# Tying indirect gathers to VectorE's message products, four to one, in a graph layer on one core

## The chip, the cores and the metric

The kernel runs on one core of one Trainium2 chip. The metric is the device time of one execution in microseconds (us). The engines are named as in the profile: PE is TensorE's matmul (PEld its weight loads), DVE is VectorE, ACT is ScalarE, POOL is GpSimd, and SP is SyncE, which only issues transfers here.

## What is computed

One message-passing layer of a graph network: 12,500 nodes of 128 features and 400,000 edges, sorted by destination. An edge's filter W comes from its length; the message is the projected source row times W; messages are summed by destination; two small matrices, a residual and a layer norm end it.

```python
rbf = jnp.exp(-(distances[:, None] - centers) ** 2 / (2.0 * width * width))
cut = 0.5 * (jnp.cos(jnp.pi * distances / CUTOFF) + 1.0) * (distances <= CUTOFF).astype(h.dtype)
W = (jax.nn.silu(rbf @ fw1 + fb1) @ fw2 + fb2) * cut[:, None]
messages = (h[src] @ pw + pb) * W
agg = jax.ops.segment_sum(messages, dst, num_segments=num_atoms)
return h + (jax.nn.silu(agg @ mw1 + mb1) @ mw2 + mb2)
...
x = _layernorm(x + _L0_gnn_ref(x, edge_index, edge_weight, ...), axis=-1)
```

Edges longer than the cutoff add nothing. The lengths go up to about 56 where the cutoff is 10, so most edges fall away.

## The kernel before

**Stages.** First the edges are packed: on VectorE, for seven chunks of the edge list, the edges beyond the cutoff are squeezed out and the rest are written to tables of sources (`srci`), destinations (`dl`) and lengths. In the first 100 us the rows of x are also projected with `pw` and stored to a table `proj` in HBM. The packing of later chunks is strewn over the next 500 us.

**Quads.** The edges that remain are worked on in 139 groups of 512, called quads here (q = 0 to 138; `NL` is 139, `QT` is 4, `QE` is 512). A quad takes:

- four **gathers** (`fetch`, line 1093, the indirect DMA at line 1099): each brings 128 source rows of 512 bytes into one quarter j of a buffer. GpSimd issues them in order. Quads 0 to 11 gather from x and are projected afterwards; from quad 12 on (`FROM_X`) they gather from `proj`.
- the **filter**: `basis` (ACT), `first` (PE, line 1167), `silu` (ACT, line 1173), `second` (PE, lines 1182 and 1185), which leaves the filter of the quad in a PSUM bank.
- the **product** (`message`, line 1189, the multiplication at line 1201): VectorE multiplies the filter by the gathered rows. It waits for the four gathers, and it frees the gather buffer and the PSUM bank.
- `place` (line 1209, the instructions at line 1214): four VectorE instructions that build the matrix that sorts edges by destination, one quad ahead.
- `sum_up` (PE, line 1235), which adds the messages by destination, and `add` (VectorE, line 1269), which puts the sums into `aggT`.

The loop at line 1593 runs over the quads; in the body, `message(q)` comes first, then `second(q + 2)`, `first`, `sum_up(q)`, `place(q + 1)` and the `add` of earlier quads. From quad 70 on the finished nodes' matmuls, statistics and stores are mixed in (`nodes`, `node_first` and so on), and the last seven quads are written out by hand from line 1668 on.

**When a gather may start.** The gather buffers are 21, and 9 from quad 63 on (`LATER`), so a gather could go as soon as the product nine quads earlier has freed its buffer. It is held back further, by a **tie**. The build counts VectorE's instructions of the kinds in `VECTORS` as they are written (`logged`, list `vectors`). `pace(q, j)` (line 449) turns a table (`PACE`) into the number of the VectorE instruction after which gather j of quad q is to start, by a straight line between the table's points and less a correction (`WERE`). Gathers that the planner has allowed stand in `queue`; `gathers()` (line 455) is called after products, after each instruction of `place` and `add` and between packing steps, and writes the first of the queue into the program once `len(vectors)` has come to its pace. `fetch` then adds a dependence on that very instruction (lines 1102 to 1105), so that GpSimd waits for VectorE to have done it. `gathers(must)` forces out what is needed for the quads below `must`: the product of quad q has `must` at q + 1, and `house(q)`, in the last seven quads, at q + 4.

Early on the table asks for a gather some 15 to 20 quads before its product; by quad 100 the distance has shrunk to about two quads, and it stays there.

Of the kernel before, what the change touches and what calls it, by code (L numbers as in the profile page):

```python
# [43 lines left out]
NL = 139  # L44
# [14 lines left out]
FIRST = 16  # L59
LISTS = 5  # L60
PACE = ((2, 17), (3, 26), (4, 36), (5, 54), (7, 95), (9, 125), (10, 144), (12, 170), (18, 250), (24, 324), (30, 373), (36, 458), (42, 544), (48, 612), (54, 691), (60, 754), (66, 826), (72, 902), (78, 982), (84, 1071), (90, 1139), (96, 1218), (102, 1306), (108, 1357), (114, 1414), (120, 1461), (126, 1518), (132, 1580), (138, 1646), (139, 1666))
VECTORS = ("TensorScalarPtr", "TensorTensor", "CopyPredicated", "TensorReduce", "TensorCopy",
           "BNStats")
SPILL = 4
# [27 lines left out]
def kernel(  # L92
# [339 lines left out]
    def place_of(q):  # L432
        n, later = LATER
        return q % len(quad_sb) if q < n else later[(q - n) % len(later)]
# [2 lines left out]

        return max((m for m in range(q) if place_of(m) == place_of(q)), default=-1)

    vectors, queue = [], []  # L440

    def logged(i):

        if i.engine == mybir.EngineType.DVE and str(i.opcode) in VECTORS:
            vectors.append(i.name)
# [3 lines left out]
    def pace(q, j):  # L449

        (a, u), (b, v) = next((k for k in zip(PACE, PACE[1:]) if q < k[1][0]))
        n = int(u + (v - u) * (q + j / QT - a) / (b - a))
        return n - sum(1 for w in WERE if w < q - 2)

    def gathers(must=0):

        while queue and (queue[0][0] < must or len(vectors) >= pace(*queue[0])):
            q, j = queue.pop(0)
            fetch(q, js=(j,))

    def room(q):

        n = q
        while n < NL and before_it(n) < q:
            n += 1
        return n

    def fetches(until, most):

        while fetched[0] < QT * min(most, known[0]) and pool[0] <= until:  # L470
            q, j = divmod(fetched[0], QT)
            if q < FROM_X:
                fetch(q, table=x, js=(j,))
            else:
                queue.append((q, j))
            if j == 0:
                pool[0] = max(pool[0], summed.get(before_it(q), 0.0))
            if j or q not in SINGLY:
                pool[0] += 1.29
            there_at[q] = pool[0] + 2.2  # L480
            fetched[0] += 1
# [5 lines left out]
    def columns(c, nodes, r_d, first, D, CAP, at_i):  # L487
# [31 lines left out]
        yield 0.6  # L519
        fetches(clock[0] + (4.0, 5.0, 5, 25)[min(c, 3)], most[0])  # L520
        gathers()
        sent.add(c)
        pool[0] = max(pool[0], clock[0]) + 1.35
# [510 lines left out]
    def own(q, name, also):  # L1034

        k = q % (4 if q >= OWN_4 else 2)
        if k > 1:
            return quad_sb[OTHERS[2 * also + k - 2]]
        if (name, k) not in own_sb:
            own_sb[name, k] = keep.tile([P, QT, H], F32, name=f"{name}{k}")  # L1040
        return own_sb[name, k]
# [51 lines left out]
    def fetch(q, idx=None, table=None, js=range(QT)):  # L1093
        got = quad_sb[place_of(q) if q >= 0 else 0]
        for j in js:
            if q in SINGLY and j == 0:
                continue
            i = srci[:, 2 * q + j // 2, j % 2:j % 2 + 1] if idx is None else idx[:, j:j + 1]
            g = nc.gpsimd.indirect_dma_start(  # L1099
                out=got[:, j, :], out_offset=None, in_=proj if table is None else table,  # L1100
                in_offset=bass.IndirectOffsetOnAxis(ap=i, axis=0))
            if PACE[0][0] <= q < NL:
                tc.add_manual_dep(
                    g.ins, vectors[min(pace(q, j), len(vectors)) - 1],
                    mybir.DependencyInfo(mybir.DependencyClass.Sync, mybir.DependencyReason.DATA))
        got_of[q] = got

# [81 lines left out]
    def message(q, js=(0, QT)):  # L1189
        gathers(q + 1)  # L1190
        msg = own(q, "msg", 0)
        a, b = js
        if q in SINGLY and a == 0:
            act = q in BY_ACT
            k = (BY_ACT if act else BY_SP).index(q)
            assert q in alone and all(s[0] != q for s in singles[act])
            nc.vector.wait_ge(row_sem[act][k % ROW_SEMS], 16 * P * (k // ROW_SEMS + 1))
            m = nc.vector.tensor_mul(msg[:, 0, :], pu_of[q][:, :H], alone.pop(q))
            tc.declare_no_dep(m.ins, group="rows", reason="waits on row_sem")
            a = 1  # L1200
        nc.vector.tensor_mul(msg[:, a:b, :], pu_of[q].rearrange("p (j f) -> p j f", j=QT)[:, a:b, :],  # L1201
                             got_of[q][:, a:b, :])
        if b == QT:
            free.append(pu_of.pop(q))
            got_of.pop(q)
        gathers()
        return msg

# [384 lines left out]
    for q in range(NL - 7):  # L1593
        while todo and q + 2 >= DIRECT // QT and todo[0] <= chunk_of(min(q + 2, NQ - 1)):
            go_on(todo[0])
        msg = message(q)
        nodes(q)
        most[0] = room(q)
# [71 lines left out]
    q = NL - 7  # L1670
    house(q)
    msg = message(q)
    second(q + 2)
    sum_up(q, msg)
# [9 lines left out]
    q += 1  # L1684
    house(q)
    msg = message(q)
    second(q + 2)
    first(octs(q - 1))
# [49 lines left out]
    p, q = NL - 2, NL - 1  # L1738
# [46 lines left out]
    def more(q):  # L1785

        fetch(-2, srci[:, 2 * q:2 * q + 2, :].rearrange("p r j -> p (r j)"))
        radial(-1, near_d[2 * q:2 * q + 2].rearrange("(o p) e -> o (p e)", o=1))
        basis(-1)
        first(-1)  # L1790
        silu(-1)
        second(-2)
        pu_of[q], got_of[q] = pu_of.pop(-2), got_of.pop(-2)
        place(q)
        msg = message(q)
        pa_of["two"] = ps.tile([P, 2, 2 * W], F32, name="sums", bufs=2)
        sum_up(q, msg)
        base_of(q)
        add(q)
# [95 lines left out]
```

## Time and profile before

| | |
|---|---|
| three runs | 941.90, 944.31, 945.89 us; median 944.31 us |
| the profiled execution | 950.38 us, of which the span from first to last instruction is 948.8 us |
| busy, PE / DVE / ACT / POOL | 663.7 / 565.9 / 398.0 / 539.2 us |
| gathers from `proj` into gather buffers | 412, of 951 ns each on POOL; 96 more, of 952 ns, into the buffers named x |
| products (line 1201) | 142 instructions, in 138 quads whole and in the last quad in four parts |
| mean granted TensorE clock | 0.808 of full speed |

A line of the timeline gives the start in us, the busy time in us, the engine, the source line, the operation, what it writes and reads, how many it stands for, and in brackets the idle time of that engine before it and what ended it. "remote" and "issue" mark waits whose end the profile can't put down to an instruction.

### The profile page before, as it was taken

The numbers are of one execution on the slowest core, as the hardware profiler recorded it, in microseconds if no ns is written. First come the engines' busy times: TensorE is split into PE (matmuls) and PEld (weight loads), VectorE is DVE, ScalarE is ACT, GpSimd is POOL, SyncE is SP. The second block draws the span as 40 slices with busy tenths as digits, with TensorE's granted clock in tenths as the row PEclk, the third lists the DMA queues.
The fourth block names the chain that finished last, engine by engine and source line by source line (L and its number), as shares of the span: only waits on it lengthen the run. The fifth ranks groups of instructions, "written<-read, shape, count | busy, mean of one in ns | idle before, by whom it ended". The sixth has DMA issues, their size and how long they took to land.

```text
span 948.8 us, 11718 instructions
## 1 busy us (share of the span) xinstructions
PE 663.7 (70%) x3531; PEld 517.3 (55%) x3531; DVE 565.9 (60%) x1725; ACT 398.0 (42%) x567; POOL 539.2 (57%) x577
## 2 busy tenths in 40 slices
PE   4663737749778867767767786868796675777656
PEld 3552535537556755655555564646575554554444
DVE  8356638745778767767678584646553344443536
ACT  4432622316335443534334433634643542454235
POOL 6346355565556656666666465546565566664661
PEclk8677767778778878888978898769987787778778
DMA  7574421232233223232324122432422342232222
GB/s 243 161 222 154 147 96 34 77 92 81 62 79 120 71 62 82 69 108 77 94 64 136 54 68 67 120 100 67 142 63 63 105 122 67 65 111 81 70 75 74
DMA packets 51295, 91.23 MB, mean 96 GB/s; under 512 B 12928, under 2 KB 18656, under 8 KB 51226
## 3 DMA queue, kind: packets, MB, share of 16 engines
q0 software_dynamic: 18096, 37.30, 15.6%
q1 hardware_dynamic: 22868, 35.09, 11.2%
q10 hardware_dynamic: 10262, 18.05, 6.0%
q8 instruction: 29, 0.48, 0.2%
q14 instruction: 40, 0.33, 0.1%
HBM read 74.59 MB, written 15.79 MB: 95 GB/s over the span
## 4 chain that ended last, share of the span: by engine, by line
PE 42%; another core or an unknown queue 16%; issue 13%; DVE 13%; ACT 10%; DVEq 1%; DMA 1%; ACTq 0%
PE ph L1167 11%; PE bank L1185 9%; PE sums L1235 9%; PE bank L348 5%; DVE hot L1214 3%; PE bank L1182 3%; PE bank L1283 2%; DVE msg L1201 2%; ACT s L1173 2%; ACT rbf L1151 2%; PE bank L1003 1%; PE bank L345 1%; ACT rbf L1155 1%; DVE aggT L1269 1%
## 5 line engine op out<-in xcount | busy, mean ns | idle before, releaser
L1099 POOL DMA_INDIRECT quad<-proj,srci x412 | 391.7, 951 | 274.0 <-issue 86.1
L1185 PEld LDWEIGHTS bank<-fw_sb,s 128*128 128x128 f32 x1112 | 177.1, 225 | 90.2 <-issue 83.6
L1173 ACT ACTIVATE s<-ph 128x1024 f32<-128x1024 f32 x70 | 71.2, 1017 | 335.6 <-PE ph L1167 159.9
L1167 PE MATMUL ph<-rbf,w_sb 102*128 102x512 f32 x278 | 164.1, 719 | 51.7 <-ACT s L1173 35.7
L1185 PE MATMUL bank<-fw_sb,s 128*128 128x128 f32 x1112 | 180.1, 310 | 22.5 <-issue 22.2
L1214 DVE TENSOR_SCALAR hot<-iota_n,dl,cut 128x80 f32<-128x80 f32 (+4 forms) x408 | 111.1, 338 | 107.0 <-PE sums L1235 49.6
L1235 PEld LDWEIGHTS sums<-hot,msg 128*128 128x128 f32 x816 | 121.5, 218 | 61.3 <-issue 40.3
L1235 PE MATMUL sums<-hot,msg 128*128 128x80 f32 (+4 forms) x816 | 122.5, 299 | 17.3 <-DVE msg L1201 10.1
L1099 POOL DMA_INDIRECT x<-proj,srci x96 | 91.4, 952 | 66.4 <-issue 21.3
L1167 PEld LDWEIGHTS ph<-rbf,w_sb 102*128 102x128 f32 x278 | 57.3, 229 | 99.7 <-issue 58.8
L1269 DVE TENSOR_TENSOR aggT<-aggT,sums 128x80 f32 (+4 forms) x209 | 53.9, 258 | 94.1 <-remote 33.8
L1182 PE MATMUL bank<-fb_b,ones_b 96*128 96x512 bf16 x139 | 60.3, 434 | 49.6 <-DVE msg L1201 15.2
L1201 DVE TENSOR_TENSOR msg<-bank,quad 128x512 f32<-128x512 f32 x78 | 53.2, 682 | 46.2 <-remote 32.7
L348 PEld LDWEIGHTS bank<-pw_sb,xT 128*128 128x128 f32 (+1 forms) x292 | 47.2, 232 | 59.0 <-issue 40.3
L1099 POOL DMA_INDIRECT quad<-in_x_dram,srci x48 | 46.3, 965 | 33.9 <-issue 12.6
L1235 PE MATMUL sums<-quad,quad 128*128 128x128 f32 (+3 forms) x296 | 49.4, 309 | 15.8 <-issue 15.2
L1151 ACT ACTIVATE rbf<-d_sb,rbf_bias,rbf_scale 102x512 f32<-102x512 f32 x70 | 56.1, 801 | 0.0
L1235 PEld LDWEIGHTS sums<-quad,quad 128*128 128x128 f32 x296 | 45.0, 225 | 20.1 <-issue 18.8
L348 PE MATMUL bank<-pw_sb,xT 128*128 128x128 f32 (+1 forms) x292 | 48.5, 319 | 6.2 <-ACT xT L1005 5.6
L345 PE MATMUL bank<-pb_b,ones_b 96*128 96x512 bf16 (+2 forms) x38 | 16.8, 443 | 46.4 <-ACT xT L1005 29.0
L1201 DVE TENSOR_TENSOR quad<-bank,quad 128x512 f32<-128x512 f32 (+1 forms) x40 | 25.9, 647 | 38.0 <-DMA quad<-proj,srci 24.2
L1005 ACT COPY xT<-bank 128x512 f32<-128x512 f32 (+1 forms) x37 | 21.3, 580 | 63.5 <-remote 49.0
(278 smaller groups left out, 881.7 us busy)
## 6 DMA issues: line engine op xcount, KB each, us to landing
d_sb<-near_d ACTq DMA_DIRECT2D x67, 256.0 KB
x<-in_x_dram SPq DMA_DIRECT2D x46, 256.0 KB
quad<-proj,srci POOLq DMA_INDIRECT x412
proj<-hp SPq DMA_DIRECT2D x24, 256.0 KB
out_dram<-x SPq DMA_DIRECT2D x22, 256.0 KB
x<-proj,srci POOLq DMA_INDIRECT x96
r_d<-in_edge_weight_dram SPq DMA_DIRECT2D x5, 256.0 KB
r_dst<-in_dst_dram SPq DMA_DIRECT2D x5, 256.0 KB
```

The costliest lines, as they stand in the source:

```text
L345: nc.tensor.matmul(to[:m, a:a + c, :], ones_b[:, :m], bias_b[:, :c, :], start=True, stop=False)
L348: nc.tensor.matmul(to[:m, k, :], lT[:, k * P:k * P + m], w, start=False, stop=(k == a + c - 1))
L1099: g = nc.gpsimd.indirect_dma_start(out=got[:, j, :], out_offset=None, in_=proj if table is None else table, in_offset=bass.IndirectOffsetO ...
L1151: a = nc.scalar.activation(rbf[:u], d[:u], AF.Square, bias=rbf_bias[:u], scale=rbf_scale[:u])
L1167: nc.tensor.matmul(ph[:, h, :], w1_sb[:2 * KR, h, :], rbf[:2 * KR], start=True, stop=True)
L1173: nc.scalar.activation(s[:, :n], ph[:, :n], AF.Silu)
L1182: nc.tensor.matmul(pu, ones_b[:, :P], bias_b["fb2"].rearrange("k j f -> k (j f)"), start=True, stop=False)
L1185: nc.tensor.matmul(pu[:, j * H:(j + 1) * H], s[:, j * P:(j + 1) * P], fw2_sb, start=False, stop=(j == QT - 1))
L1201: nc.vector.tensor_mul(msg[:, a:b, :], pu_of[q].rearrange("p (j f) -> p j f", j=QT)[:, a:b, :], got_of[q][:, a:b, :])
L1214: nc.vector.tensor_scalar(hot[:, j, :wide(q)], iota_n[:, :wide(q)], dl[:, at[0], at[1]], cut[:, at[0], at[1]], op0=OP.is_equal, op1=OP.mult)
L1235: nc.tensor.matmul(pa[:, k * W:k * W + wide(q)], msg[:, j, :], hot[:, j, :wide(q)], start=(j % n == 0), stop=(j % n == n - 1))
L1269: nc.vector.tensor_add(to, to, pa[:, k * W:k * W + wide(q)])
```

## The change

A gather is no longer tied to the VectorE instruction that its pace names, but to a product. The build keeps a list `products` with the count of VectorE instructions at each whole product. With `HALF = 6`, a gather of pace n is written into the program as soon as the last product's count is at least n - 6, or, if none has come by then, when n + 6 instructions have been written. It is tied to the first product whose count is at least n - 6, or, where there is none yet, to the last product before. Gathers written before the first product get no tie; these are the ones for quads 2 to 11, whose ties to early instructions fall away. Everything else stays: the table, the correction, the planner, the order of the gathers, their buffers and VectorE's instructions.

```diff
+HALF = 6
...
-    vectors, queue = [], []
+    vectors, queue, products = [], [], []
...
     def gathers(must=0):
-        while queue and (queue[0][0] < must or len(vectors) >= pace(*queue[0])):
+        while queue and (queue[0][0] < must or products[-1:] >= [pace(*queue[0]) - HALF]
+                         or len(vectors) >= pace(*queue[0]) + HALF):
             q, j = queue.pop(0)
             fetch(q, js=(j,))
+
+    def tied_to(q, j):
+
+        n = pace(q, j) - HALF
+        return vectors[next((k for k in products if k >= n), products[-1]) - 1]
...
-            if PACE[0][0] <= q < NL:
+            if PACE[0][0] <= q < NL and products:
                 tc.add_manual_dep(
-                    g.ins, vectors[min(pace(q, j), len(vectors)) - 1],
+                    g.ins, tied_to(q, j),
                     mybir.DependencyInfo(mybir.DependencyClass.Sync, mybir.DependencyReason.DATA))
...
         if b == QT:
             free.append(pu_of.pop(q))
             got_of.pop(q)
+            products.append(len(vectors))
         gathers()
```

## The prediction, made before the changed kernel was run

> **What bounds the kernel now.** I read the page first, then the waits of the product, then the waits of PE in the stage where gathers come latest, then single stretches of the timeline.
>
> ```profile
> PE 663.7 (70%) x3531; PEld 517.3 (55%) x3531; DVE 565.9 (60%) x1725; ACT 398.0 (42%) x567; POOL 539.2 (57%) x577
> PEclk8677767778778878888978898769987787778778
> PE 42%; another core or an unknown queue 16%; issue 13%; DVE 13%; ACT 10%; DVEq 1%; DMA 1%; ACTq 0%
> L1099 POOL DMA_INDIRECT quad<-proj,srci x412 | 391.7, 951 | 274.0 <-issue 86.1
> ```
>
> PE leads the chain that ended last, with 42%. POOL is idle 43% of the span, so the ties hold the gathers back, not its speed. DMA has 1% of the chain. Whether a tie matters must show at the products, so I asked what they wait for. Up to quad 98 the rows land long before: the last gather of quad 97 and its product are
>
> ```profile
> 669.14 0.94 POOL L1099 DMA_INDIRECT quad<-proj,srci  x1 [0.30 <-issue]
> 680.16 0.68 DVE L1201 TENSOR_TENSOR msg<-bank,quad 128x512 f32<-128x512 f32 x1
> ```
>
> 11.0 us apart, the least of quads 12 to 98. From quad 99 on they come close. The view of line 1201 from 690 to 870 us (quads 100 to 127):
>
> ```profile
>   DMA quad<-proj,srci: 26.1, 11
> who waited for it (us, times):
>   POOL quad L1099: 9.8, 8
> ```
>
> The longest waits of PE in the same stretch:
>
> ```profile
> PE sums L1235 <- issue: 14.8, 13, 2.4
> PE bank L1185 <- issue: 12.7, 9, 2.3
> PE ph L1167 <- ACT s L1173: 5.0, 1, 5.0
> ```
>
> And busy times by stretches (PE, PEld, DVE, ACT, POOL; then granted clock, DMA share and GB/s):
>
> ```profile
> 690.00:870.00 180.00, 132.19 (x687) 102.74 (x686) 78.64 (x259) 79.56 (x109) 105.55 (x113) 0.81 0.30 87
> 712.00:721.00 9.00, 2.44 (x9) 1.54 (x8) 0.67 (x3) 3.55 (x5) 4.81 (x6) 0.66 0.34 103
> 721.00:734.00 13.00, 13.00 (x67) 10.04 (x68) 7.91 (x28) 4.29 (x5) 7.86 (x9) 0.84 0.15 37
> 797.00:810.00 13.00, 12.93 (x70) 10.13 (x70) 7.78 (x25) 1.62 (x2) 8.80 (x10) 0.88 0.16 42
> ```
>
> This is the heart of it. Eleven products wait 26.1 us for gathers, yet nobody but POOL itself waits for those products: PE does not. PE alternates between stretches in which it is full (13.00 of 13 us) and halts in which it waits for nothing that the profile names (2.44 of 9 us, at a granted clock of 0.66). VectorE is busy 78.64 of 180 us and runs ahead of PE in both.
>
> **The change part by part.** I worked out each gather's tie from the code and the count of VectorE's instructions: 508 gathers from quad 12 on, now tied to 492 different instructions, would hang on 135 products; 298 would be free over 0.3 us earlier than now, 142 over 0.3 us later, 0.8 us earlier in the mean.
>
> *Waits on POOL.* A gather keeps one wait whatever it is tied to:
>
> ```profile
> L1099 POOLq EVENT_SEMAPHORE  x113: 17/17/17, 690.5 to 868.3; - x113
> ```
>
> 17 ns each, and gathers one behind another start 0.94 + 0.30 = 1.25 us apart with it. Gain taken: 0.
>
> *The start.* The first product is at 121.6 us. Gathers of quads 12 to 16 that now begin at 104.7 us would wait for it, 18 hang on it, and POOL needs 18 x 1.25 = 22.5 us to catch up. The first of them and the product of quad 12:
>
> ```profile
> 104.74 0.94 POOL L1099 DMA_INDIRECT quad<-proj,srci  x1 [3.47 <-DMA proj<-hp]
> 237.98 0.67 DVE L1201 TENSOR_TENSOR msg<-bank,quad 128x512 f32<-128x512 f32 x1
> ```
>
> 133 us of cover: 0. Without it, 17 us. The seven packing scatters on POOL's queue wait for nothing new: a gather ahead of one is tied to a product that VectorE does before the scatter's own data. From there to quad 98 no gather would start more than 5.4 us later than it does, against a cover of 11.0 - 2.7 = 8.3 us at least (2.7 is start to product, below): 0.
>
> *Quads 99 to 133.* Here I took VectorE's times as they stand and gave each gather the later of two starts: 1.25 us after the gather before it, or 0.3 us after its product's end. The product can start 2.7 us after the last gather's start, as in the first and third rows here:
>
> ```profile
> 727.45 0.94 POOL L1099 DMA_INDIRECT quad<-proj,srci  x1 [0.30 <-issue]
> ...
> 730.16 0.69 DVE L1201 TENSOR_TENSOR quad<-bank,quad 128x512 f32<-128x512 f32 x1 [4.82 <-DMA quad<-proj,srci]
> 730.16 1.04 PE L1235 MATMUL sums<-hot,msg 128*128 128x104 f32 x8
> ```
>
> Nine products would come later: quads 101 (0.4), 105 (2.0), 113 (0.9), 115 (0.7), 117 (2.0), 118 (0.4), 119 (1.1), 121 (1.0) and 125 (0.5), 9.0 us in all. About as many would come up to 0.7 us earlier, 2.4 us in all. The two largest show the pattern, a last gather that moves from an instruction before a pair of products to the first of the pair:
>
> ```profile
> 717.39 0.94 POOL L1099 DMA_INDIRECT quad<-proj,srci  x1 [0.30 <-issue]
> 721.03 0.69 DVE L1201 TENSOR_TENSOR msg<-bank,quad 128x512 f32<-128x512 f32 x1 [8.29 <-remote]
> 722.61 0.69 DVE L1201 TENSOR_TENSOR msg<-bank,quad 128x512 f32<-128x512 f32 x1
> 727.33 0.38 PE L1182 MATMUL bank<-fb_b,ones_b 96*128 96x512 bf16 x1
> ...
> 793.37 0.94 POOL L1099 DMA_INDIRECT quad<-proj,srci  x1 [0.30 <-issue]
> 797.24 0.69 DVE L1201 TENSOR_TENSOR msg<-bank,quad 128x512 f32<-128x512 f32 x1 [7.94 <-remote]
> 798.89 0.68 DVE L1201 TENSOR_TENSOR msg<-bank,quad 128x512 f32<-128x512 f32 x1
> 804.04 0.38 PE L1182 MATMUL bank<-fb_b,ones_b 96*128 96x512 bf16 x1
> ```
>
> Quad 105's last gather has pace 1328 and starts at 717.39; its new tie is instruction 1330, the product of quad 104, done at 721.7. So it starts at 722.0, and the product at 724.7 instead of 722.61. What is late next? `second` of quad 107, at 727.33, which needs the bank that this product frees at 723.3: 4.0 us of slack for 2.0 us. At quad 117 it is 804.04 - 799.6 = 4.5 us for 2.0. The other seven have 2.3 us or more for at most 1.1. So PE covers all nine. Taken: 0; bounds -2.4 and +9.0 us, if PE had no slack.
>
> *VectorE beside the gathers.* Releases would fall on `place`, which often follows the product. Rows of both kinds, each with the gather that starts during it or just before:
>
> ```profile
> 475.25 1.10 DVE L1214 TENSOR_SCALAR hot<-iota_n,dl,cut 128x112 f32<-128x112 f32 x4
> 475.60 0.94 POOL L1099 DMA_INDIRECT quad<-proj,srci  x1 [1.74 <-DVE hot L1214]
> ...
> 748.69 1.06 DVE L1214 TENSOR_SCALAR hot<-iota_n,dl,cut 128x104 f32<-128x104 f32 x4
> 749.28 1.04 POOL L1099 DMA_INDIRECT quad<-proj,srci  x1 [4.66 <-DVE hot L1214]
> 750.26 1.34 DVE L1214 TENSOR_SCALAR quad<-iota_n,dl,cut 128x104 f32<-128x104 f32 x4
> 750.62 0.94 POOL L1099 DMA_INDIRECT quad<-proj,srci  x1 [0.30 <-DVE quad L1214]
> ```
>
> 475.60 is a gather that is tied to a product already: `place` took 1.10 us, 0.04 above 1.06. The worst case is 1.34, 0.28 above. With 135 releases and VectorE's 13% of the chain: 135 x 0.04 x 0.13 = 0.7 us, at most 135 x 0.28 x 0.13 = 4.9, at least 0 (as many may hit it now). Taken: 0.7, since the row at 475 is the very case.
>
> [...]
>
> *The end.* From quad 134 on gathers are forced out and would be tied 4 us or more earlier, with cover either way. Quad 129's product waits 1.79 us for its rows; its last gather would start 0.3 us earlier, and PE did wait there:
>
> ```profile
> 878.15 0.69 DVE L1201 TENSOR_TENSOR msg<-bank,quad 128x512 f32<-128x512 f32 x1 [1.79 <-DMA quad<-proj,srci]
> 878.90 0.38 PE L1182 MATMUL bank<-fb_b,ones_b 96*128 96x512 bf16 x1 [0.22 <-DVE msg L1201]
> ```
>
> Taken: -0.3, bounds -1.8 and 0.
>
> *The sum.* 0 + 0 + 0 + 0.7 - 0.3 = +0.4 us on the profiled execution's 950.38 us. That execution lies 6.1 us (0.6%) above the median of the runs; carried over to the median, 944.31 + 0.4 is 944.7 us, no change. What this kernel's measurement can tell from no change is about 0.5%, 4.7 us.
>
> **The rivals.**
>
> *Slower: bursts reach PE.* One release now frees up to four gathers, which POOL takes 1.25 us apart; where the last two or three of a quad hang on the product just before its own, that product can't come until 0.3 + 2 x 1.25 + 2.7 = 5.5 us after it. It decides from the point where PE's slack at a product is under 2 us. Against it: the slacks above. For it: they are measured after halts of PE that need not fall at the same places, and a shift of their phase could put a late product where there is none. Without any slack the nine delays give 944.3 + 9.0 = 953.3 us; with the earlier ones set off, 950.9. I name 951.
>
> *Slower still: a late product leaves PE idle, and its clock drops.* At 0.66 of the clock in 712 to 721, and with `second`'s first matmul at
>
> ```profile
> 722.19 0.63 PE L1182 MATMUL bank<-fb_b,ones_b 96*128 96x512 bf16 x1
> ```
>
> 0.63 us against 0.38 at 727.33, ten slow microseconds cost some 4. Two such stretches, beside the two delays of 2.0: 944.3 + 12 = 956 us. [...]
>
> *Faster: earlier releases shorten the eleven waits.* If PE's slack were only apparent and each wait shrank by the mean 0.8 us, 8.8 us would go: 935.5 us. Against it: for the last gathers of those very quads the ties move by -1.3 to +2.6 us, with no gain on balance.
>
> *The change does not do what it says:* 135 ties for 508 gathers say it does.
>
> **How the numbers follow.** Forecast, all hidden: 0.50. Bursts reach PE: 0.25. Clock: 0.07. Faster: 0.18. The forecast's own range is 940 to 949.5, the bounds of its small terms; a tenth of it spills beyond 0.5% on either side. Faster 0.18 + 0.02 = 0.20, slower 0.32 + 0.03 = 0.35, same 0.45. For 8 in 10 the range takes in the burst case whole and the faster one in part: 937 to 955 us. I name 945.
>
> **What would show it.** Right: POOL's gathers in groups of three or four, 1.25 us apart behind a product; the products of the second of a pair waiting for DMA more often; PE in 690 to 870 us still not waiting for line 1201, and busy about 132 us there. Wrong: PE (lines 1182, 1235) waiting for line 1201 there by 5 us or more (bursts), a granted clock below 0.80 (clock), or the products' DMA waits well under 26 us together with a shorter stretch (faster).

## The result, and the profile after

| | kernel before | changed kernel |
|---|---|---|
| median of 4 runs | 944.67 us (941.90 to 945.89) | 999.61 us (998.20 to 1001.53) |
| ratio | | 1.0587, interval 1.0556 to 1.0619 |
| span of the profiled execution | 948.8 us | 997.0 us |

The forecast was 945 us, no change, within 937 to 955. The changed kernel is 55 us slower, outside of that range and beyond every rival. Some runs of a kernel are in a slower state than the rest; ratios here and below leave them out, and medians don't.

From the page of the changed kernel: busy times, the chain that ended last, and the group of the gathers (busy us and mean ns of one, then idle us before them).

```profile
PE 670.0 (67%) x3531; PEld 521.9 (52%) x3531; DVE 566.2 (57%) x1725; ACT 398.2 (40%) x567; POOL 539.9 (54%) x577
PE 38%; another core or an unknown queue 18%; issue 14%; DVE 13%; POOL 6%; ACT 5%; DVEq 1%; DMA 1%; ACTq 0%; POOLq 0%
L1106 POOL DMA_INDIRECT quad<-proj,srci x412 | 391.1, 949 | 313.7 <-issue 131.5
```

The engines have hardly more work: PE 670.0 us against 663.7, POOL 539.9 against 539.2. The added time is idle time. POOL is new in the chain with 6%, and the gathers' idle time rose from 274.0 to 313.7 us.

Where it went shows in two long windows (busy times of PE, PEld, DVE, ACT, POOL with the instructions in brackets, then clock, DMA share and GB/s). Before:

```profile
120.00:520.00 400.00, 286.08 (x1501) 225.00 (x1499) 277.06 (x744) 157.63 (x198) 240.32 (x253) 0.80 0.29 82
520.00:900.00 380.00, 280.13 (x1452) 212.56 (x1453) 190.56 (x645) 167.16 (x234) 218.81 (x232) 0.82 0.30 85
```

After:

```profile
120.00:520.00 400.00, 255.54 (x1342) 201.72 (x1341) 242.10 (x648) 138.74 (x172) 224.17 (x235) 0.76 0.24 72
520.00:900.00 380.00, 286.74 (x1472) 217.27 (x1471) 205.84 (x671) 171.02 (x239) 221.71 (x234) 0.82 0.30 90
```

From 120 to 520 us the changed kernel gets through 1342 of PE's matmuls where the kernel before gets through 1501. The 159 that are missing are 42 us of work at the old pace (400 x 159 / 1501), of the 48.2 us between the spans. From 520 to 900 us nothing is lost (1472 against 1452). Quad against quad it is the same: the first product comes 0.9 us later than before (121.86 against 120.93), that of quad 51 43.0 us later (468.5 against 425.5), that of quad 132 39.1 us later, and the end 48.2 us later. So the loss falls up to quad 51, and a second one of 9 us behind quad 132, which is shown below. The first window is where VectorE still packs chunks of the edge list, and where the prediction had found large covers.

What POOL waited for in that window. Before:

```profile
POOL quad L1099 <- DVE hot L1214: 34.9, 26, 6.9
POOL quad L1099 <- DVE quad L1201: 3.1, 1, 3.1
POOL quad L1099 <- DVE msg L1201: 3.0, 5, 1.7
POOL x L1099 <- DVE msg L1201: 0.9, 1, 0.9
```

After (in all, times, the longest):

```profile
POOL quad L1106 <- issue: 57.8, 108, 13.0
POOL quad L1106 <- DVE msg L1208: 46.6, 9, 24.0
POOL x L1106 <- DVE msg L1208: 27.8, 6, 8.4
```

POOL now stands 74.4 us waiting for products (46.6 + 27.8), where it stood 7.0 us (3.1 + 3.0 + 0.9) and waited for `place` and the packing. Where the row says "issue", some of it is a wait for a product too: of POOL's 32 idle times over 0.4 us in this window, 30 end 0.27 or 0.74 us behind the end of a product, and they make 127.7 of 135.0 us (before: 9 of 57, and 10.5 of 99.8 us). So its gathers come in fewer and longer runs: 32 with 7.3 gathers in the mean, where there were 58 with 4.3. Here is one turn of the timeline of the changed kernel, from a product at 199 us to one at 242.

```profile
199.25 0.68 DVE L1208 TENSOR_TENSOR msg<-bank,quad 128x512 f32<-128x512 f32 x1
...
200.67 0.94 POOL L1106 DMA_INDIRECT quad<-proj,srci  x1 [13.04 <-issue]
...
228.36 0.59 PE L346 MATMUL bank<-pb_b,ones_b 96*128 96x512 bf16 x1 [10.66 <-issue]
...
231.46 0.95 POOL L1106 DMA_INDIRECT quad<-proj,srci  x1 [0.30 <-issue]
...
236.11 0.59 ACT L1032 COPY quad<-bank 128x512 f32<-128x512 f32 x1 [7.80 <-remote]
236.75 0.59 PE L1189 MATMUL bank<-fb_b,ones_b 96*128 96x512 bf16 x1 [6.09 <-ACT quad L1032]
...
242.63 0.67 DVE L1208 TENSOR_TENSOR msg<-bank,quad 128x512 f32<-128x512 f32 x1
...
244.04 0.94 POOL L1106 DMA_INDIRECT quad<-proj,srci  x1 [11.63 <-issue]
```

POOL idles 13.04 us and starts 0.7 us behind the product's end. It then runs 25 gathers with no gap over 0.6 us, the last at 231.46. In that run PE stands 10.66 us ("issue": it waits for nothing that the profile shows) and then 6.09 us for a copy of ScalarE, which had stood still itself; it is at work again at 236.75, 4.3 us after the last gather's end. The next product that POOL acts on comes at 242.63, and POOL, idle for 11.63 us, starts 0.7 us behind its end. Each engine waits out the other.

The kernel before has the same sight in a smaller size; its longest early run of gathers, 17 of them, ends with the first row here:

```profile
133.62 0.94 POOL L1099 DMA_INDIRECT x<-proj,srci  x1 [0.30 <-issue]
...
137.43 0.59 PE L345 MATMUL bank<-pb_b,ones_b 96*128 96x512 bf16 x1 [14.88 <-ACT xT L1005]
```

The run that stands in its place in the changed kernel, 22 gathers that waited for the first product:

```profile
122.82 0.94 POOL L1106 DMA_INDIRECT quad<-proj,srci  x1 [23.97 <-DVE msg L1208]
...
149.04 0.94 POOL L1106 DMA_INDIRECT x<-proj,srci  x1 [0.30 <-issue]
...
154.03 0.58 PE L1189 MATMUL bank<-fb_b,ones_b 96*128 96x512 bf16 x1 [21.35 <-ACT xT L1012]
```

The loss at the end looks the same. The products of quads 132 and 133, before:

```profile
899.88 0.69 DVE L1201 TENSOR_TENSOR msg<-bank,quad 128x512 f32<-128x512 f32 x1
904.93 0.68 DVE L1201 TENSOR_TENSOR msg<-bank,quad 128x512 f32<-128x512 f32 x1
```

After, with what lies between them:

```profile
939.02 0.69 DVE L1208 TENSOR_TENSOR msg<-bank,quad 128x512 f32<-128x512 f32 x1
...
952.70 0.94 POOL L1106 DMA_INDIRECT quad<-proj,srci  x1 [0.30 <-issue]
...
953.86 0.58 PE L1189 MATMUL bank<-fb_b,ones_b 96*128 96x512 bf16 x1 [13.59 <-issue]
...
958.43 0.68 DVE L1208 TENSOR_TENSOR msg<-bank,quad 128x512 f32<-128x512 f32 x1
```

The row at 952.70 is the last of 22 gathers in one run that began at 926.49. In the kernel before, the longest run here has 13 gathers, and PE's halt, of 9.80 us, comes behind quad 133. When both are past, at the product of quad 137, the lag has grown from 39.1 to 47.5 us.

How much of the loss lies in such halts can be counted. Take as a run gathers with less than 0.4 us between them, and of each run the part from 10 us after its start to 4 us behind its end. From 120 to 520 us PE is busy in 36% of that time in the kernel before (73.0 us in all) and in 19% in the changed kernel (92.1 us). Its idle time there goes from 46.5 to 74.2 us, which is 27.7 of the 30.5 us that PE's idle time grows by in the whole window; with 12 and 3 us in place of 10 and 4 it is 23.3. In the first 10 us of a run PE is busy in some 80%, before and after.

So the halts of PE, of which the prediction quoted one at 712 to 721 us and took them as given, go with long runs of back-to-back gathers (the one at 712 begins 11 us into a run of 14). Whether the gathers make the halts was the thing to test.

### The profile page after: what moved, and what is told of

It is laid out like the page before. It is cut to its first block, busy times and chain, and to the rows that moved or that the text cites. A ratio compares the mean times of both kernels' runs of the same rounds, so it can differ in the third digit from the quotient of the medians.

```text
span 997.0 us, 11375 instructions
## 1 busy us (share of the span) xinstructions
PE 670.0 (67%) x3531; PEld 521.9 (52%) x3531; DVE 566.2 (57%) x1725; ACT 398.2 (40%) x567; POOL 539.9 (54%) x577
## 4 chain that ended last, share of the span: by engine, by line
PE 38%; another core or an unknown queue 18%; issue 14%; DVE 13%; POOL 6%; ACT 5%; DVEq 1%; DMA 1%; ACTq 0%; POOLq 0%
PE ph L1174 9%; PE bank L1192 9%; PE sums L1243 8%; POOL quad L1106 6%; PE bank L349 4%; DVE hot L1222 3%; PE bank L1189 2%; DVE msg L1208 2%; PE bank L1291 2%; DVE aggT L1277 1%; PE bank L1010 1%; PE bank L346 1%; DVE bank L552 1%; DVE nodes L556 1%
## 5 line engine op out<-in xcount | busy, mean ns | idle before, releaser
L1106 POOL DMA_INDIRECT quad<-proj,srci x412 | 391.1, 949 | 313.7 <-issue 131.5
L1192 PEld LDWEIGHTS bank<-fw_sb,s 128*128 128x128 f32 x1112 | 180.4, 229 | 135.6 <-issue 125.0
L1192 PE MATMUL bank<-fw_sb,s 128*128 128x128 f32 x1112 | 182.2, 314 | 17.4 <-issue 17.3
L1174 PE MATMUL ph<-rbf,w_sb 102*128 102x512 f32 x278 | 161.2, 703 | 34.4 <-ACT s L1180 24.4
L1243 PEld LDWEIGHTS sums<-hot,msg 128*128 128x128 f32 x816 | 122.8, 218 | 79.1 <-issue 56.7
L1243 PE MATMUL sums<-hot,msg 128*128 128x80 f32 (+4 forms) x816 | 127.1, 300 | 33.1 <-issue 18.9
L1106 POOL DMA_INDIRECT x<-proj,srci x96 | 91.6, 954 | 65.3 <-DVE msg L1208 27.8
L1243 PE MATMUL sums<-quad,quad 128*128 128x128 f32 (+3 forms) x296 | 46.8, 305 | 14.8 <-DVE quad L1208 8.3
L1293 ACT ACTIVATE zs<-bank 128x512 f32<-128x512 f32 (+2 forms) x27 | 15.0, 555 | 83.7 <-remote 28.3
```

Source lines behind the costliest of these rows:

```text
L1106: g = nc.gpsimd.indirect_dma_start(out=got[:, j, :], out_offset=None, in_=proj if table is None else table, in_offset=bass.IndirectOffsetO ...
L1174: nc.tensor.matmul(ph[:, h, :], w1_sb[:2 * KR, h, :], rbf[:2 * KR], start=True, stop=True)
L1192: nc.tensor.matmul(pu[:, j * H:(j + 1) * H], s[:, j * P:(j + 1) * P], fw2_sb, start=False, stop=(j == QT - 1))
L1243: nc.tensor.matmul(pa[:, k * W:k * W + wide(q)], msg[:, j, :], hot[:, j, :wide(q)], start=(j % n == 0), stop=(j % n == n - 1))
```

## The experiments

The runs came in six groups, each on one chip and with its own runs of the kernel before. On the chips of four groups the kernel before takes about as long as in the first runs, on those of two groups far less. A ratio is always to the kernel before of the same group.

| group | kernel before (runs) | kernels |
|---|---|---|
| 1 | 734.5 us (13) | engines' streams, start undone, start alone |
| 2 | 955.5 us (7) | changed kernel, engines' streams, start undone |
| 3 | 737.2 us (13) | fours, products late, both kernels with a pause |
| 4 | 942.5 us (7) | changed kernel, fours, products late, before with a pause |
| 5 | 958.3 us (7) | products early, changed kernel with a pause |
| 6 | 955.3 us (7) | before with a short pause, changed kernel |

Below, chips "with halts" are those of groups 2, 4, 5 and 6. No chip was in two groups, so that it goes with the chip, and not with the occasion, is not shown.

### One engine's stream beside gathers

A kernel of its own, with the whole computation left out. `begin` gates each stretch with VectorE; no instruction of a stream waits for a gather.

```python
for k in range(28):
    gather(k)          # the indirect DMA, 128 rows of 512 bytes
fast(400)              # 400 matmuls 128x128 by 128, f32
...
slow(70)               # the same beside 70 matmuls with 512 columns
...
    nc.vector.tensor_copy(dv[:, 0:1], dv[:, 1:2])   # 400 times
...
    nc.scalar.copy(ac[:, 0:1], ac[:, 1:2])          # 200 times
...
    gather(k)
    nc.gpsimd.memset(scratch[:, 0:256], 0.0)
```

> This kernel leaves the whole computation out. It runs nine stretches, each begun by VectorE: short matmuls alone, then one engine's stream beside 28 gathers back to back: short matmuls, long matmuls, VectorE copies, ScalarE copies; then short matmuls beside gathers with a memset of 256 elements after each, beside groups of eight gathers with a memset of 2048 behind each, beside 28 gathers of 128-byte rows, beside 40 gathers of half the rows. In the profiles of both kernels TensorE's instructions come 0.7 to 1.4 us apart from about the ninth of a run of back-to-back gathers, 9 to 13 us after its start, until about 3.5 us after its last; by then TensorE has issued 115 to 135 matmuls and weight loads in that run. Theory by gathers: the ninth decides, so the halt comes at 10 to 11 us with short and with long matmuls alike. Theory by instructions: an engine lives on a stock of about 128 that isn't refilled while gathers run, so the short matmuls (0.11 us, with a weight load each) halt after some 7 us, the long ones (0.5 us or more) after 30 us or not at all, VectorE's and ScalarE's copies after about 128 of them. By both, groups of eight with a long pause don't halt; by the theory by gathers a short pause after each doesn't either. Theory that neither holds (the kernel's own waits make the halts): no stretch halts, and 400 short matmuls take about 44 us.

> The nine stretches of the engines' streams beside gathers again, with the computation left out. Where the kernel before takes about 735 us: as in the first run of this kernel, no stretch halts, 28 gathers take 35 us and 400 short matmuls 44.5 us. Where it takes about 944: the theories as written for the first run; by gathers both kinds of matmuls halt from the ninth gather on, by instructions the short ones after 115 to 135 instructions and the long ones much later.

Group 1, without halts: 847.9 us. Windows over the gathers (in order: short matmuls after 9 us, long matmuls, VectorE, ScalarE, short matmuls with the memset):

```profile
71.00:97.00 26.00, 26.00 (x235) 26.00 (x234) 0.00 (x0) 0.00 (x0) 19.08 (x21) 1.00 0.19 53
...
174.00:198.00 24.00, 24.00 (x57) 10.64 (x56) 0.00 (x0) 0.00 (x0) 17.93 (x19) 1.00 0.18 52
...
249.00:269.00 20.00, 0.00 (x0) 0.00 (x0) 16.33 (x106) 0.00 (x0) 15.10 (x16) 0.50 0.19 53
...
333.00:353.00 20.00, 0.00 (x0) 0.00 (x0) 0.00 (x0) 17.20 (x90) 15.12 (x17) 0.50 0.18 53
...
375.00:403.00 28.00, 28.00 (x253) 28.00 (x252) 0.00 (x0) 0.00 (x0) 24.85 (x40) 1.00 0.16 46
```

Group 2, with halts: 1021.5 us. The first row is the stretch of short matmuls up to the ninth gather, the second its rest. Two rows of the long matmuls follow, then two of VectorE and two of ScalarE (the first 15 us beside gathers, then the place as above), then the short matmuls with the memset, and last a stretch of short matmuls beside groups of eight gathers with a memset of 1.83 us behind each group:

```profile
60.00:71.00 11.00, 11.00 (x83) 10.96 (x82) 0.00 (x0) 0.00 (x0) 8.53 (x9) 0.83 0.17 49
71.00:95.00 24.00, 6.00 (x21) 4.68 (x19) 0.00 (x0) 0.00 (x0) 18.03 (x20) 0.56 0.18 52
...
189.00:200.00 11.00, 10.86 (x21) 4.74 (x22) 0.19 (x2) 0.00 (x0) 8.10 (x9) 0.80 0.16 46
200.00:224.00 24.00, 24.00 (x58) 10.61 (x57) 0.00 (x0) 0.00 (x0) 18.21 (x20) 1.00 0.19 53
...
262.00:277.00 15.00, 0.00 (x0) 0.00 (x0) 12.20 (x80) 0.00 (x0) 10.74 (x12) 0.50 0.15 44
277.00:297.00 20.00, 0.00 (x0) 0.00 (x0) 3.99 (x26) 0.00 (x0) 15.12 (x17) 0.50 0.18 52
...
366.00:381.00 15.00, 0.00 (x0) 0.00 (x0) 0.64 (x5) 12.90 (x68) 10.80 (x12) 0.50 0.16 45
381.00:401.00 20.00, 0.00 (x0) 0.00 (x0) 0.00 (x0) 5.28 (x28) 15.12 (x17) 0.50 0.18 53
...
440.00:468.00 28.00, 22.75 (x134) 19.99 (x133) 0.00 (x0) 0.00 (x0) 24.86 (x39) 0.79 0.16 47
...
579.00:612.00 33.00, 26.04 (x181) 23.19 (x179) 0.00 (x0) 0.00 (x0) 26.41 (x26) 0.90 0.16 47
```

And how it ends, in the same profile's timeline:

```profile
93.88 0.94 POOL L42 DMA_INDIRECT got<-in_x_dram,idx  x1 [0.30 <-issue]
...
99.56 8.62 PE L48 MATMUL bank<-b,gate 128*128 128x128 f32 x54 [0.33 <-issue]
```

Short matmuls that wait for nothing run freely for 11 us and 165 records (83 + 82), and then almost stop: 40 records in 24 us, where the other chip has 469 in 26. They run freely again 5.7 us after the last gather's start. VectorE and ScalarE fall in the same way, from 106 to 26 and from 90 to 28 in 20 us. The long matmuls don't halt: up to 224 us, when the gathers end, they have issued 158 records (21 + 22 + 58 + 57). So it isn't the ninth gather that decides: the halt comes after some 11 us for short matmuls, 15 us for the copies, and not in 35 us for long matmuls. In these streams short matmuls and copies get a number of records out beside back-to-back gathers, and then one in 0.6 to 0.8 us (24 us / 40, 20 us / 28, 20 us / 26). That is the theory by instructions in kind, but not in its number: PE's 165 lie above its 115 to 135, and VectorE and ScalarE halt after some 80 and 70, where it had about 128. (Nor do the 115 to 135 hold for every run in the kernels: runs of twelve or more gathers in the first profiles of both kernels have 61 to 134 records of PE and PEld in their first 10 us, and 0 to 52 from there to 4 us behind their end.) The stock that this theory names is shown by no row. Both theories had no halt beside groups of eight with a long pause, and both miss there: PE gets 360 records (181 + 179) in 33 us, where the other chip gives 595. Gathers of 128-byte rows cost PE as much (119.4 us from the first of 400 short matmuls to the last, against 119.8 with whole rows; 92 both times on the other chip, and not 44, since the profile has two matmul records for each, 4900 for 2450), so it isn't the bytes moved here. A memset of 0.33 us behind each gather, which widens the gap between two gathers on POOL from 0.31 to 0.50 us, lets 267 records through in 28 us, where the other chip has 505.

### The start

```diff
         n = pace(q, j) - HALF
+        if pace(q, j) <= products[0]:
+            return vectors[pace(q, j) - 1]
```

This is the changed kernel with the old ties for quads 12 to 16. The start alone is the kernel before with `max([pace(q, j), *products[:1]])` in place of `pace(q, j)`.

> The changed kernel, but the 18 gathers whose pace lies at or below the first product (quads 12 to 16) keep the tie that they had before, so that they run from 105 us on and not in a run of 22 from 122.8 us. Theory of the start (those gathers are late, and all after them): nearly all of the 55 us comes back, 945 to 955 us, with the product of quad 12 at about 238 us. Theory of the bursts (runs of more than nine gathers halt TensorE, wherever they come): the halt of 21 us at 132 goes back to the 13.6 us of before, and with it what it pushes on; the runs after it stay, so 975 to 992 us.

> The kernel before, with the gathers of quads 12 to 16 whose pace lies below the first product held to the first product, and every other tie as before. Theory of the start: 990 to 1000 us. Theory of the bursts: one run of about 18 to 22 gathers in place of one of 17, its halt 7 to 20 us longer, all else as before: 952 to 966 us.

Group 1: the start undone 736.2 us, 1.0011 (0.9990 to 1.0032); the start alone 746.5 us, 1.0165 (1.0112 to 1.0217). No halts there, so neither theory was put to the test, but the kernel is another one on such a chip: POOL hardly ever waits and sets the end: in the profile of the start undone its 577 instructions, most of them 1.25 us apart, are 721 us of a span of 734.5. There the start costs what it leaves POOL idle, 11.58 us in the profile of the start alone. In the part of the runs that was counted above, from 10 us after a run's start on, PE is busy in 83% on this chip (550 us of 120 to 700, start undone): back-to-back gathers don't halt it here.

The pair on a chip with halts:

> The changed kernel as it is. In the runs of the start undone the kernel before took 734.5 us and showed no halt of TensorE, in the first runs 944 us with halts; so the halts are of where or when a kernel runs. Without halts, POOL's gathers run back to back there through nearly the whole span (577 instructions at 1.25 us are 721 us of 734), and the 18 gathers held to the first product cost what they leave idle on POOL: 746 to 752 us, 1.5 to 2.5% over before, and nothing more for the ties in fours. With halts: 998 to 1002 us against 944 as in the first runs.

> The changed kernel with the old ties for the 18 gathers at or below the first product's pace, again. Without halts: as before within 0.5% (1.0011 the first time). With halts: theory of the start 945 to 955 us, theory of the bursts 975 to 992 us.

Group 2: the changed kernel 1011.5 us, 1.061 (1.054 to 1.068); the start undone 1009.3 us, 1.056 (1.048 to 1.063). The theory of the start falls: with it undone nothing measurable comes back. The theory of the bursts had 975 to 992, and is missed as well: other runs of gathers took the place of the one at 122.8 us. PE's idle time late in runs, counted as above, is 79.3 us in this group's changed kernel and still 74.9 with the start undone. The start alone wasn't run on a chip with halts.

### Fours, or products

Two ways in which the ties could do it. Fours on any instruction, in the kernel before:

```diff
-        n = int(u + (v - u) * (q + j / QT - a) / (b - a))
+        n = int(u + (v - u) * (q + 1.5 / QT - a) / (b - a))
```

and the changed ties from quad 54 on alone (`FROM_PRODUCT = 54`, with `gathers` split in the same way):

```diff
+        if q < FROM_PRODUCT:
+            return vectors[min(pace(q, j), len(vectors)) - 1]
         n = pace(q, j) - HALF
```

> The kernel before with the four gathers of a quad tied to one VectorE instruction, whichever stands at the quad's mean pace, and not to a product. Theory of the loop (a gather tied to a product hangs, through that product, on TensorE's `second`, which the last burst of gathers has just halted; a packing instruction hangs on nothing of TensorE's): fours as such cost little, 945 to 965 us where the kernel before takes 950, within 1%. Theory of the fours (groups of four make longer runs, and longer runs halt TensorE, whatever they hang on): 985 to 1010 us. Where the kernel before takes 735 us POOL is never idle for long: within 0.5% by both.

> The changed kernel with its ties for quads 54 on, and the old ones, one instruction to a gather, for all quads ahead of it. In the traces the products of the changed kernel fall behind by 40 us up to quad 51, while VectorE packs, and by nothing from there to quad 132. Theory of the loop: little is lost late, where there is no packing left and a tie to another instruction hangs on TensorE as well: 950 to 965 us where the kernel before takes 950. Theory of the fours: the loss goes with the gathers, 340 of 508, some 35 us: 980 to 995. Where the kernel before takes 735: within 0.5%.

Group 3, without halts: fours 746.0 us, 1.0119 (1.0101 to 1.0136), which neither theory had (within 0.5%) and whose cause stays open; products late 736.2 us, 0.9987 (0.9972 to 1.0001).

> The changed kernel as it is, a third time. Where the kernel before takes some 950 us: 1.055 to 1.07 of it again. Where it takes some 735 us the changed kernel hasn't run yet: the start undone gave 1.0011 there and the start alone 1.0165, so by the sum of both 1.012 to 1.02, all of it from the 18 gathers at the start.

> The fours on any VectorE instruction again (the kernel before, a quad's four gathers on one instruction at its mean pace). Where the kernel before takes 737 us it gave 1.0119, with POOL never idle for long. Where it takes some 950: theory of the loop 945 to 965 us, theory of the fours 985 to 1010, as written for the first run.

> The changed ties from quad 54 on alone, again (0.9987 where the kernel before takes 737 us). Where it takes some 950: theory of the loop 950 to 965 us, theory of the fours 980 to 995.

Group 4, with halts: the changed kernel 1006.0 us, 1.067 (1.059 to 1.076); fours 971.7 us, 1.025 (1.017 to 1.034); products late 960.2 us, 1.017 (1.009 to 1.024). Fours cost something as such, less than half of the whole; that lies between the two theories, above the 1% that the loop's allowed and below the 985 us for 950 of the other. The late ties cost 1.7%, at the edge of what the theory of the loop had for them. Some of it is the loss at the end: from the product of quad 132 to that of quad 137, 41.0 us pass in the profile of late ties alone and 42.6 to 46.8 in the four of the changed kernel, against 34.2 in the kernel before. The counterpart, the changed ties up to quad 53 alone:

> The changed ties for the quads ahead of 54 alone, and the old ones from quad 54 on. On the chip where the kernel before takes 942 us the changed kernel took 63 us more, ties from quad 54 on alone 18, fours on any instruction 29, and in its profile the fours lost nothing up to quad 56, where the changed kernel had lost 36. Theory of the loop (ties to products cost while VectorE packs): 975 to 1000 us where the kernel before takes some 945, 1.035 to 1.06. Theory of the fours alone: 1.00 to 1.01. Where the kernel before takes 737: 1.01 to 1.02 (the start).

Group 5: 989.7 us, 1.036 (1.027 to 1.044). That is 31 us, at the low edge of what was expected, and 3.55% + 1.65% is 5.2%, about the whole (5.9 to 6.8%), though from two chips. From quad 132 to 137 early ties alone take 34.5 us, as before. The windows say where the rest is. Products late, then products early:

```profile
120.00:520.00 400.00, 276.74 (x1455) 219.19 (x1455) 270.05 (x721) 154.76 (x194) 233.90 (x245) 0.79 0.26 76
```

```profile
120.00:520.00 400.00, 269.65 (x1347) 211.12 (x1347) 247.05 (x660) 140.52 (x173) 223.24 (x235) 0.75 0.24 72
```

With early ties to products alone, PE does 1347 matmuls up to 520 us, as few as in the changed kernel (1342); with late ones alone 1455. (The 1501 of the kernel before are of another chip.) Idle time in the late parts of runs isn't a price by itself: counted as above it is 68.7 us with late ties alone, where PE idles less outside of them, and 75.1 us with early ones.

### A pause behind each gather

```diff
+            if q >= 0:
+                nc.gpsimd.memset(rest, 0.0)
```

`rest` is a tile of 256 elements in each partition that nothing reads; the memset follows each gather on POOL, in the kernel before and in the changed kernel.

> The kernel before with a memset of 256 elements on POOL behind each gather (0.33 us; period 1.44 in place of 1.25 us). In the stretches with the engines' streams this cut the halt of TensorE beside 28 gathers from 28 to 17 us. Theory of the starved engines (engines get next to no instructions while POOL writes gathers back to back): 850 to 920 us where the kernel before takes 950; where it takes 735 and no engine starves, POOL bounds it, 556 x 0.19 = 106 us more, 835 to 845. Theory that the halts are the kernel's own waits: POOL comes later everywhere, 955 to 1000.

> The changed kernel with the same memset behind each gather. Theory of the loop: with the halts shorter the loop through TensorE costs less, so 10 to 30 us over the kernel before with the memset. Theory of the fours: with the gaps between gathers back, the runs do no harm, 0 to 12 us over it (the 18 gathers of the start). If neither gap nor halt matters, 50 to 60 us over it. Where the kernel before takes 735: 10 to 20 us over it.

Group 3: 850.6 and 852.0 us, 1.154 and 1.155. Where nothing halts the pause costs 113.4 us, about the 556 x 0.19 = 106 us by which POOL is longer, and with it the change costs 1.4 us, where 10 to 20 were expected.

> The kernel before with the memset behind each gather, again (850.6 us where the kernel before takes 737, POOL's own pace). Where it takes some 950: theory of the starved engines 850 to 920 us, so faster than before there; theory that the halts are the kernel's own waits 955 to 1000.

> The changed kernel with the memset behind each gather, again (1.1548 where the kernel before takes 737 us, beside 1.1540 for the kernel before with it). Where the kernel before takes some 945, the kernel before with the memset took 878. Theory of the loop through a halted TensorE: with the halts shorter, the loop costs less than the 63 us that it cost without the memset, so 885 to 915 us. If the halts have no part in the loss: 935 to 945.

Group 4: the kernel before with the pause 878.5 us, 0.933 (0.926 to 0.940), 64 us faster than the kernel before without it. Slower on POOL made the kernel faster; that the halts are the kernel's own waits is out. In its profile POOL is busy 727.7 us (84%) and waits 3.4 us for products.

Group 5: the changed kernel with the pause 930.2 us, 0.976 (0.967 to 0.984). Its waits of POOL:

```profile
POOL quad L1107 <- DVE msg L1211: 26.4, 9, 15.9
POOL quad L1107 <- DVE quad L1211: 21.1, 9, 6.7
POOL x L1107 <- DVE msg L1211: 12.1, 4, 4.3
```

Between these two lie 0.976 / 0.933 = 1.046, where the kernels without the pause lie 1.059 to 1.068 apart. The loop had 885 to 915 us, no part of the halts 935 to 945: neither is met. The interval of the 1.046, worked out from those of both ratios, is some 1.034 to 1.058, from two chips: shorter halts don't take the loss away, and that they lessen it is hardly clear of the noise. Another cost has come in besides: with the pause POOL is the busiest engine (84% in the kernel before, 79% in the changed one), and the changed kernel makes it wait 59.6 us for products.

> The kernel before with a memset of 128 elements behind each gather in place of 256 (0.20 in place of 0.33 us by the row of the memset of ident; period some 1.32 in place of 1.44). With 256 the gathers took 556 x 1.44 = 802 us of 869, POOL was hardly idle (32 us) and set the end. Theory that engines are fed in the gaps between gathers, by the length of the gap: a gap shorter by 0.12 us feeds them less, and POOL's floor is 67 us lower; between 840 and 900 us where the kernel before takes some 945. If the gap must pass some length: no better than 920. Where the kernel before takes 737: POOL's pace, 556 x 0.07 to 0.12 more, 775 to 805.

> The changed kernel as it is. Where the kernel before takes 737 us it hasn't run yet: 1.012 to 1.02 by the start alone (1.0165) and the start undone (1.0011), with POOL idle for some 12 us at the first product and nowhere else. Where the kernel before takes some 950: 1.055 to 1.07, as in three calls before.

Group 6: with 128 elements 935.6 us, 0.987 (0.974 to 0.999); the changed kernel 1010.2 us, 1.068 (1.053 to 1.082). The memsets of 128 elements take 225 ns each, those of 256 (group 4) 333 ns. With 0.17 us of idle time behind them these make gaps of 0.39 and 0.50 us in place of 0.31. The first step of 0.08 us brings 1.3% (0.1 to 2.6), the second of 0.11 us another 5.4%; by the length alone the first would bring 2.8% of the 6.7. That fits the expectation that the gap must pass some length ("no better than 920"), but it rests on two lengths, each on its own chip, and is not shown.

## Why the prediction was wrong, point by point

**What bounds the kernel.** "PE alternates between stretches in which it is full (13.00 of 13 us) and halts in which it waits for nothing that the profile names." The rows were right, and the reading stopped one question short: what do the other engines do when a halt begins? The quoted rows at 717.39 and 793.37 are gathers with the least gap, 0.30 us, inside halts. The halts were taken as PE's own, so that gathers could act on PE through their rows alone. The streams of group 2 show the other way: beside back-to-back gathers short matmuls and copies that wait for nothing slowed down after some 70 to 165 records (PE from 165 in 11 us to 40 in 24).

**The start, "133 us of cover: 0", and the quads up to 98, "against a cover of 11.0 - 2.7 = 8.3 us at least (2.7 is start to product, below): 0".** This is the step that failed. As to rows it was right: from 120 to 520 us no product of either kernel waits for rows. But 42 of the 48 us are lost there, where the step had 0. The 5.4 us by which no gather was to be later took VectorE's times as they stand, and the products came up to 43 us later themselves. The cover counted the slack of a gather's rows against its own product, and left out what a burst does to PE meanwhile, and that POOL's waits for products (74.4 us against 7.0) turn gathers that ran beside other work into such bursts: PE's idle time late in runs grew by 27.7 us in this window. The start isn't needed for it (1.056 with it undone, 1.061 with it): the ties of the other quads cost about as much without it. With all early ties, start included, it is 1.036.

**Quads 99 to 133: 0, bounds -2.4 and +9.0.** From 690 to 870 us the waits of quads 100 to 127 for their rows had been 26.1 us in 11 times. In the changed kernel these quads lie at 735 to 910 us, and the view of the product's line has

```profile
  DMA quad<-proj,srci: 33.5, 14
```

and PE's own waits there have

```profile
PE sums L1243 <- DVE quad L1208: 3.9, 1, 3.9
PE sums L1243 <- DVE msg L1208: 2.5, 1, 2.5
PE bank L1189 <- DVE msg L1208: 0.9, 1, 0.9
```

The rows came 7.4 us later in all, where the step had 9.0 - 2.4 = 6.6, and PE does wait for products now, 7.3 us. That was named as the sign of the bursts. But the 28 quads take no longer than before (169.8 us from first product to last, against 170.7), so the 0 that was taken came out in this profile, though not for its reason, that PE covers every late product. Late ties alone cost 1.7%, 16 us of 942.5; a part of that is the end.

**VectorE beside the gathers: +0.7.** No sign of more: a gather's mean is 949 ns against 951, and gathers start 0.27 us behind their product, while `place` runs (122.82 and 275.15, for two).

**Waits on POOL: 0.** Nothing speaks against it: gathers are 1.25 us apart as before.

**The end: -0.3, "with cover either way".** This failed too, and in the same way. The rows were there: the product of quad 133 comes 20.7 us after its last gather's start. But the forced gathers joined those ahead of them into the run of 22, PE stood still for 13.59 us beside it, and the lag grew by some 9 us.

**The rivals.** "Bursts reach PE" had the word and not the way: it let bursts act through late rows, with 9 us at most, at quads 99 to 133. The clock is lower, 0.76 against 0.80 in the window that loses, but PE's busy time as a whole rose by 6.3 us only, so it is a small part. Nothing spoke for the rival that ended faster. Of the signs, gathers in groups behind a product came as said, and so did more products that wait for DMA; the others looked at 690 to 870 us, where nothing was lost.

What the runs settle: on chips with halts the ties to products of the early quads make most of the loss, the late ones the rest. Where nothing halts they cost nothing but the start (1.0011 without it; the changed kernel itself didn't run on such a chip). That doesn't set the halts apart by itself, since POOL is behind its ties there: its longest wait for a product is 2.1 us. With halts shortened they cost 4.6%. The reading is that POOL, tied to products that PE must first feed, idles while PE could have borne gathers, and then runs them back to back just when PE has work. The single links are measured: POOL's idle times end at products, its runs are longer, PE's idle time grows in the late parts of long runs, and a stream that waits for nothing halts beside such gathers. That they make up the whole 55 us is not shown term by term, and the start undone, which brought next to nothing back, shows that the loop's parts can't be added up.

## What to carry to other kernels

A halt in which an engine waits for nothing is a question, not a given: list what every other engine does at its start, first of all GpSimd's transfers (PE's halt of 10.66 us here fell into a run of 25 gathers). A tie to an instruction ties to all that this instruction waits for, so a pace is best tied to work that doesn't hang on the engine that the paced transfers disturb. And a slack measured for one consumer says nothing of the others: cover must be counted for each resource that a burst uses.

## What the runs showed of the hardware that was not expected

- The same kernel takes 734.5 and 737.2 us on two chips and 942.5 to 958.3 us on the chips of four other groups. On the first two POOL sets the end (its 577 instructions, most 1.25 us apart, are 721 us of 734.5 in the profile of the start undone, and none of its waits is over 3.2 us in that of the fours); on the others PE idles late in runs of gathers (68.7 to 79.3 us from 120 to 520 us in four profiles of groups 2, 4 and 5), and the streams, which ran on one of them, halt. What sets the two apart is not known.
- On the chip of group 2, PE's stream all but stops after 165 records beside gathers that are 1.25 us apart (40 in the next 24 us), and VectorE's and ScalarE's fall, after some 80 and 70, to about a quarter and a third (26 records in 20 us against 106 on the chip of group 1, and 28 against 90). Short matmuls come back to back again 5.7 us after the last gather's start, at a granted clock of 0.52 from 99 to 105 us.
- 0.33 us of other work on POOL behind each gather made the kernel before 6.7% faster there and 15.4% slower where nothing halts.
- What is scarce in a halt wasn't seen. The queues named "instruction" carry the same packets with and without halts (39 and 8 in both profiles of the streams). Every timed execution was also recorded, so that a part of the recording in the halts isn't excluded.
